# Issuing the next group's row products between the chunks of the present group's 5x5 convolution

## The chip, the cores and the metric

One core of one Trainium2 chip runs the whole program. The metric is device time in microseconds. The core is alone in the program, and the spread of one kernel's runs is about 0.2 %. PE is the matmul engine, PEld its weight loads, DVE the vector engine, ACT the scalar engine, POOL the GpSimd engine, SP the engine that issues loads.

## The reference, cut to what matters

The program is four layers: a row LSTM, an adder network, a Hartley transform, and an encoder-decoder. The change touches the encoder of the last layer, which handles 16 images of 32 channels in four groups of four images (one 32-partition block each):

```
b1 = norm(0.5 * corr(x, SOBEL_X) + 0.5 * corr(x, SOBEL_Y))     # and four more edge operators, b2 ... b5
y  = conv3x3(concat([b1, b2, b3, b4, b5]), conv1_w, conv1_b)   # 160 channels in, 32 out
y  = maxpool2(y)
y  = conv2 -> pool -> conv3 -> pool -> conv4 -> deconv1 -> conv5 -> deconv2 -> conv6 -> ...
```

`norm` divides by a standard deviation over the whole image. The kernel therefore needs the statistics of five filtered images before it can convolve. It never makes these images: their variances follow from products of rows of x with neighbouring rows (here "row products"). Filters, norms and conv1 are then folded into one 5x5 convolution with 32 input channels, plus corrections along the edges.

## The kernel before

The parts that the argument touches (cuts marked with [...]):

```python
def edge_statistics(nc, pool, ps, cst, gm, frames, g):
    gram = [ps.tile([128, 512], F32, name="acc") for _ in range(4)]      # four accumulator banks
    [...]
    for ch in range(H // 16):                                            # 8 chunks of 16 rows
        xp = frames.chunk(g, ch)
        for l in range(2, 18):                                           # row products: 16 small matmuls a row
            [...]
                    nc.tensor.matmul(gram[blk][...], xp[rows, l, ...], xp[rows, l : l + n, ...], ...)
    [...]                                                                # then DVE: es_w, es_red, means, deviations
    return mean, inv_sqrt(nc, pool, var, 5, 0.0), sides

def fold_operators(nc, pool, ps, cst, w1, mean, istd, bias):
    [...]
    for n, (...) in PARTS.items():              # n: all, t, tl, tr, b, bl, br, l, r
        t = pool.tile([128, h * w + 1, 32], F32, name=f"fo_{n}")
        nc.gpsimd.memset(t, 0.0)                                         # L634
        [...]                                   # some 170 small DVE instructions (L647, L650)
    b = pool.tile([128, 4], F32, name="fo_b")
    p = [ps.tile([128, 512], F32, name="acc") for _ in range(4)]         # four more banks
    [...]                                                                # bias products into p (L659)
    for blk in range(4):
        nc.vector.tensor_tensor(b[:, blk : blk + 1], p[blk][:, :1], bias[:, 0:1], ALU.add)   # L663
    return out, b

# encoder: fp has bufs=2, ps has bufs=8 (all eight banks, one name)
ready = prepared(0)                             # statistics and fold of group 0
for g in range(NG):
    sides, wf, b1 = ready
    if g + 1 < NG:
        ready = prepared(g + 1)                 # statistics and fold of the next group, before this convolution
    [...]                                       # side products, then `cut`
    for ch in range(H // R):                    # the 5x5 convolution, 8 chunks of 800 matmuls (L814)
        acc = [ps.tile([128, 512], F32, name="acc") for _ in range(4)]
        [...]                                   # then DVE and ACT add `cut`, pool, add the bias: the eviction
    conv_pool(y1, 64, "conv2", 1, y2)           # conv2 to conv6, with deconv1 and deconv2 between
    [...]
```

A buffer pool here has a set of buffers for each name: a tile waits until the tile that held its buffer before, under the same name, has had its last reader.

## Time and profile before

| | before |
|---|---|
| time, median of 3 runs | 9529.88 us (9524.95 to 9548.11) |
| profiled run | 9529.85 us, span 9528.1 us |
| encoder, from its first loads to the end of conv6 of the last group | 6738 to 8905.4 us of the span (first row product at 6765.7) |
| preparation before the first convolution | 386.1 us |
| group 0: from its convolution to the next one | 548.6 us |
| group 3: convolution, then conv2 to conv6 | 221.3 us, 87.0 us |

From the page of the kernel before: the span, two of the slice rows (tenths of busy time, tenths of full clock), and the two groups of PE instructions that the change moves (count, then busy us and mean ns, then the idle time just before them and what ended it):

```profile
span 9528.1 us, 263499 instructions
...
PE   4999979999999999999999999857549677689877
...
PEclk9999989999999999999999999555559688789888
...
L814 PE MATMUL acc<-xp,fo_all 32*32 32x512 f32 x25600 | 931.1, 624 | 55.2 <-DVE pooled L718 48.1
...
L559 PE MATMUL acc<-xp 32*32 32x108 f32 x16384 | 321.1, 370 | 260.1 <-issue 228.3
```

The row products (L559) are busy 321 us and cost another 228 us in which PE waited for nothing but its own instructions ("issue"). The convolution (L814) waits 48 us for pooling. Slices 26 to 30 run at half clock; the last two of them, from 6738 us on, are the preparation ahead of the first convolution. Slice 32, at 0.6, holds the next row products.

### The profile page before, as it was taken

The page shows a single profiled execution, that of the slowest core. Times are in us where ns is not written, and L with a number is a line of the kernel's source. Part 1 is how long each engine was busy: PE and PEld are TensorE (multiplying, and loading weights), DVE is VectorE, ACT ScalarE, POOL GpSimd, SP SyncE. Part 2 cuts the span into 40 slices and gives each one's busy share as a digit, 9 for nine tenths or more (in the row PEclk, how much of TensorE's full clock was granted, in tenths as well). Part 3 has the DMA queues.
Part 4 walks back from the last instruction along what each step waited for, and adds up shares of the span by engine and source line. Part 5 has one row for each costly group of instructions (what it writes and reads, how often), then busy time and mean ns, then how long its engine had stood idle before and what let it go on. Part 6 is the DMA issues. An engine that isn't in the chain of part 4 may idle for free.

```text
span 9528.1 us, 263499 instructions
## 1 busy us (share of the span) xinstructions
PE 8174.5 (86%) x122202; PEld 5240.3 (55%) x122202; DVE 6188.6 (65%) x7704; ACT 5079.5 (53%) x3286; POOL 478.9 (5%) x585
## 2 busy tenths in 40 slices
PE   4999979999999999999999999857549677689877
PEld 4888864544445444444544444856436455457544
DVE  5444439999999999999999999315252232322333
ACT  1444329989899898989989899000001101011200
POOL 0111110000000000000000000000000000000122
PEclk9999989999999999999999999555559688789888
DMA  9899930000000000000000000527411111111333
GB/s 193 61 80 80 61 55 1 19 19 19 19 10 11 19 19 19 20 19 1 19 19 20 19 10 7 161 48 229 145 52 41 55 35 46 46 30 34 103 119 112
DMA packets 1530826, 494.30 MB, mean 52 GB/s; under 512 B 1420028, under 2 KB 1423612, under 8 KB 1522172
## 3 DMA queue, kind: packets, MB, share of 16 engines
q1 hardware_dynamic: 1474588, 364.48, 23.3%
q10 hardware_dynamic: 55136, 112.95, 3.3%
q8 instruction: 957, 15.68, 0.7%
q14 instruction: 145, 1.19, 0.0%
HBM read 330.59 MB, written 146.80 MB: 50 GB/s over the span
## 4 chain that ended last, share of the span: by engine, by line
DVE 41%; PE 38%; issue 14%; DMA 3%; SPq 2%; ACT 1%; POOL 1%; DVEq 0%; ACTq 0%; POOLq 0%
DVE d_dve L317 34%; PE acc L814 9%; PE pg L179 4%; PE pg L180 4%; PE acc L559 3%; PE acc L705 3%; PE pg L181 2%; PE p L379 2%; PE acc L300 2%; PE acc L932 2%; PE pf L479 1%; PE acc L906 1%; DMA out_dram<-xo 1%; DVE xc L332 1%; PE acc L323 1%
## 5 line engine op out<-in xcount | busy, mean ns | idle before, releaser
L323 PE MATMUL acc<-d_dve,sel 128*32 128x512 f16 x27648 | 3994.0, 379 | 44.0 <-DVE d_dve L317 44.0
L323 PEld LDWEIGHTS <-sel 128*32 128x32 f16 x36864 | 2042.8, 95 | 2056.1 <-issue 218.4
L314 ACT ACTIVATE d_act<-qa,neg 128x4096 f16<-128x4096 f16 x768 | 2803.0, 3697 | 131.8 <-PE acc L323 131.1
L317 DVE TENSOR_SCALAR d_dve<-qa,qw 128x4096 f16<-128x4096 f16 x2304 | 2790.3, 1284 | 111.1 <-PE acc L323 86.5
L323 PE MATMUL acc<-d_act,sel 128*32 128x512 f16 x9216 | 2182.2, 380 | 0.0
L314 ACT ACTIVATE d_act<-qb,neg 128x4096 f16<-128x4096 f16 x384 | 1419.2, 3696 | 0.0
L317 DVE TENSOR_SCALAR d_dve<-qb,qw 128x4096 f16<-128x4096 f16 x1152 | 1411.4, 1284 | 0.0
L814 PE MATMUL acc<-xp,fo_all 32*32 32x512 f32 x25600 | 931.1, 624 | 55.2 <-DVE pooled L718 48.1
L814 PEld LDWEIGHTS acc<-xp,fo_all 32*32 32x32 f32 x25600 | 664.5, 105 | 313.8 <-issue 162.9
L179 PE MATMUL pg<-h,bd 128*128 128x256 f32 x2048 | 651.7, 400 | 59.8 <-DVE h L199 59.5
L190 ACT ACTIVATE gt<-pg,bias 128x256 f32<-128x256 f32 x1024 | 400.9, 474 | 546.1 <-PE pg L181 545.9
L180 PE MATMUL pg<-h,bd 128*128 128x256 f32 x2048 | 622.3, 386 | 0.0
L729 ACT ACTIVATE y<-pooled,fo_b 32x128 f32<-32x128 f32 x256 | 102.4, 400 | 841.0 <-DVE pooled L718 837.6
L559 PE MATMUL acc<-xp 32*32 32x108 f32 x16384 | 321.1, 370 | 260.1 <-issue 228.3
L842 DVE TENSOR_TENSOR acc<-acc,cut 128x4 f32<-128x4 f32 x256 | 28.7, 166 | 698.1 <-PE acc L814 697.1
L181 PE MATMUL pg<-xn,bd 128*128 128x2 f32 (+62 forms) x2048 | 425.6, 289 | 10.7 <-DVE xn L163 10.7
L181 PEld LDWEIGHTS pg<-xn,bd 128*128 128x128 f32 x2048 | 396.1, 194 | 67.6 <-DVE xn L163 11.5
L559 PEld LDWEIGHTS acc<-xp 32*32 32x32 f32 x16384 | 246.6, 133 | 334.3 <-issue 275.2
L180 PEld LDWEIGHTS pg<-h,bd 128*128 128x128 f32 x2048 | 397.9, 194 | 56.8
L194 DVE TENSOR_TENSOR c<-c,gt 128x256 f32<-128x256 f32 x256 | 108.5, 424 | 447.7 <-ACT gt L190 447.7
L530 DVE TENSOR_SCALAR xp<-xp,stats 128x2560 f32<-128x2560 f32 (+1 forms) x64 | 101.1, 1580 | 457.6 <-DMA xp<-x_d 457.6
L179 PEld LDWEIGHTS pg<-h,bd 128*128 128x128 f32 x2048 | 341.2, 195 | 66.8 <-issue 49.9
(233 smaller groups left out, 5879.5 us busy)
## 6 DMA issues: line engine op xcount, KB each, us to landing
xp<-x_d SPq DMA_DIRECT2D x48, 1280.0 KB
x_in<-in_x_dram SPq DMA_DIRECT2D x16, 2048.0 KB
res<-in_x_dram SPq DMA_DIRECT2D x32, 1024.0 KB
x_d<-res SPq DMA_DIRECT2D x32, 1024.0 KB
x_d<-xc ACTq DMA_DIRECT2D x16, 2048.0 KB
xr<-x_d SPq DMA_DIRECT2D x32, 1024.0 KB
x_d<-xr ACTq DMA_DIRECT2D x32, 1024.0 KB
xr<-x_d SPq DMA_DIRECT2D x128, 256.0 KB
```

The costliest lines, as they stand in the source:

```text
L179: nc.tensor.matmul(pg[:, q], wmat(0, q), h_in[:, :, 1:], start=True, stop=False)
L180: nc.tensor.matmul(pg[:, q], wmat(1, q), h_in[:, :, :H], start=False, stop=False)
L181: nc.tensor.matmul(pg[:, q, :, : t + 1], wmat(2, q), xn[:, 2 * c : 2 * c + 2, j, : t + 1], start=False, stop=True,)
L190: nc.scalar.activation(gt[:, q], pg[:, q], AF.Tanh if q == 3 else AF.Sigmoid, bias=bias[:, q : q + 1])
L300: nc.tensor.matmul(acc[k][32 * j : 32 * j + 32, :], sel16[:, 8, :], window(tap)[:, 4 * k : 4 * k + 4, :], start=tap == 0, stop=False,)
L314: nc.scalar.activation(d, window(tap), AF.Relu, bias=neg[:, i : i + 1])
L317: nc.vector.tensor_scalar(d, window(tap), qw[:, i : i + 1], 0.0, ALU.subtract, ALU.max)
L323: nc.tensor.matmul(acc[k][32 * j : 32 * j + 32, :], sel16[:, f8, :], ds[j][:, 4 * k : 4 * k + 4, :], start=False, stop=f8 == 7 and tap == 8,)
L379: nc.tensor.matmul(p1[:, i, :], xh[:, 16 * half + i, :], cst["cas"], start=True, stop=True)
L559: nc.tensor.matmul(gram[blk][32 * j : 32 * j + 32, at : at + 36 * n], xp[rows, l, 2 + 32 * j : 34 + 32 * j], xp[rows, l : l + n, 32 * j : ...
L705: nc.tensor.matmul(acc[blk][32 * j : 32 * j + 32, : rows * n], wc[name][part, tap, :], src[part, at : at + rows, kw : kw + n], start=tap == 0,
L814: nc.tensor.matmul(acc[blk][32 * j : 32 * j + 32, :], wf["all"][rows, tap, :], xp[rows, 4 * j + kh : 4 * j + kh + 4, kw : kw + W], start=t ...
```

## The change

The intent: the row products of the next group need only x, so they can be spread between the chunks of this group's convolution. PE then has work while a chunk is evicted, and the convolution of a group need not wait until the next group has been prepared. For this the row products get four banks of their own ("gram"), and the other tiles keep four ("acc").

```diff
-def edge_statistics(nc, pool, ps, cst, gm, frames, g):
+def edge_statistics(nc, pool, ps, cst, gm, frames, g, out):
-    gram = [ps.tile([128, 512], F32, name="acc") for _ in range(4)]
+    gram = [ps.tile([128, 512], F32, name="gram") for _ in range(4)]
[... in the loop over chunks, after a chunk's row products:]
+        yield
[... the statistics' and the fold's other PSUM tiles: "acc" -> "gram"]
-    return mean, inv_sqrt(nc, pool, var, 5, 0.0), sides
+    out.update(mean=mean, istd=inv_sqrt(nc, pool, var, 5, 0.0), sides=sides)
[...]
-        ps = ctx.enter_context(tc.tile_pool(name="e_ps", bufs=8, space=PSUM))
+        ps = ctx.enter_context(tc.tile_pool(name="e_ps", bufs=4, space=PSUM))
[...]
-            if g + 1 < NG:
-                ready = prepared(g + 1)
+            following = Operators(g + 1) if g + 1 < NG else None
[... after each chunk of the convolution:]
+                if following:
+                    following.step()
+            if following:
+                ready = following.folded()
             conv_pool(y1, 64, "conv2", 1, y2)
```

`Operators` holds the generator. `step()` issues one chunk of row products. `folded()` runs what is left (the statistics, then the fold), after the whole convolution.

More of the change, by code (lines that the diff above doesn't have):

```diff
@@ L589, in edge_statistics @@
         nc.vector.tensor_reduce(red[:, blk, :], w, AX.X, ALU.add)
-    p = ps.tile([128, 512], F32, name="acc")
+    p = ps.tile([128, 512], F32, name="gram")
     nc.tensor.matmul(p[:, :20], cst["ones"], red[:, 0:4, :].rearrange("p b k -> p (b k)"), start=True, stop=True)
@@ L595, in edge_statistics @@
     nc.vector.tensor_reduce(sq, own.rearrange("p b k -> p k b"), AX.X, ALU.add)
-    q = ps.tile([128, 512], F32, name="acc")
+    q = ps.tile([128, 512], F32, name="gram")
     nc.tensor.matmul(q[:, :5], cst["avg32_bc"], red[:, 4, :], start=True, stop=True)
@@ L654, in fold_operators @@
     b = pool.tile([128, 4], F32, name="fo_b")
-    p = [ps.tile([128, 512], F32, name="acc") for _ in range(4)]
+    p = [ps.tile([128, 512], F32, name="gram") for _ in range(4)]
     for j in range(4):
@@ L766, in deconv, with __init__, step, folded @@
                     )
-        def prepared(g):
-            mean, istd, sides = edge_statistics(nc, fp, ps, cst, gm, frames, g)
-            return sides, *fold_operators(nc, fp, ps, cst, w1, mean, istd, bias)
-        ready = prepared(0)
+        class Operators:
+            def __init__(self, g):
+                self.out = {}
+                self.steps = edge_statistics(nc, fp, ps, cst, gm, frames, g, self.out)
+            def step(self):
+                next(self.steps, None)
+            def folded(self):
+                for _ in self.steps:
+                    pass
+                o = self.out
+                return o["sides"], *fold_operators(nc, fp, ps, cst, w1, o["mean"], o["istd"], bias)
+        ready = Operators(0).folded()
         for g in range(NG):
             sides, wf, b1 = ready
-            if g + 1 < NG:
-                ready = prepared(g + 1)
+            following = Operators(g + 1) if g + 1 < NG else None
             cps = [ps.tile([128, 512], F32, name="acc") for _ in range(4)]
```

## The prediction

> **What bounds the kernel now.** I read the page's slices first. The change touches only the encoder, slices 29 to 37; the 40 slices are 238 us each, and everything before 6738 us and after 8905 us of the span is the same code in both kernels. Then I cut the encoder into its stages with the table by windows (PE's busy time, then the granted clock):
>
> ```profile
> 6738.00:7124.06 386.06, 174.51 (x8968) 0.50 0.27 76
> 7124.06:7386.34 262.28, 245.93 (x6736) 0.92 0.14 37
> 7386.34:7480.52 94.18, 77.95 (x2042) 0.84 0.06 17
> 7480.52:7621.73 141.21, 79.03 (x4110) 0.55 0.29 82
> 7621.73:7672.65 50.92, 9.87 (x742) 0.50 0.10 28
> ...
> 8597.07:8818.41 221.34, 214.72 (x6745) 0.99 0.10 27
> 8818.41:8905.39 86.98, 73.70 (x2040) 0.86 0.01 3
> ```
>
> From the top: row products and folding of groups 0 and 1; the 5x5 convolution of group 0; its conv2 to conv6; the row products of group 2 (141 us, PE half busy at half clock); their tail (51 us, PE nearly idle). The last two lines are the 5x5 convolution and conv2 to conv6 of group 3, which has no follower. So a group takes 548.6 us (7124.06 to 7672.65), 192 of them preparation that PE could partly do elsewhere. That is what the change is after. Two things in the table are odd: the row products run at half clock, and the convolution of group 3 is 41 us shorter than that of group 0. The timeline of PE explains both. Row products (start, us, then the idle time before):
>
> ```profile
> 7485.00 1.77 PE L559 MATMUL acc<-xp 32*32 32x108 f32 x128 [1.84 <-issue]
> 7489.02 1.77 PE L559 MATMUL acc<-xp 32*32 32x108 f32 x128 [2.25 <-issue]
> ...
> 7508.66 2.55 PE L559 MATMUL acc<-xp 32*32 32x108 f32 x128 [1.19 <-issue]
> ...
> 8046.42 2.54 PE L559 MATMUL acc<-xp 32*32 32x108 f32 x128 [5.56 <-issue]
> ...
> 8059.30 2.54 PE L559 MATMUL acc<-xp 32*32 32x108 f32 x128 [0.93 <-issue]
> ```
>
> Every 128 matmuls (256 instructions with their weight loads) PE stops. At full clock 128 take 1.77 us, at half clock 2.54, but the period is the same, 3.5 to 3.75 us: a faster clock only lengthens the stop. The row products are bound by the supply of instructions, not by the array. The long stops (3 to 5.6 us) coincide with loads of xp.
>
> The 5x5 convolution (800 matmuls a chunk), group 0, then what holds its banks:
>
> ```profile
> 7189.08 1.88 PE L814 MATMUL acc<-xp,fo_all 32*32 32x512 f32 x18 [1.26 <-DVE pooled L718]
> ...
> 7192.08 28.92 PE L814 MATMUL acc<-xp,fo_all 32*32 32x512 f32 x782 [1.12 <-DVE pooled L718]
> ...
> 7394.78 0.35 DVE L663 TENSOR_TENSOR fo_b<-acc,bias 128x1 f32<-128x1 f32 x4
> ```
>
> Each chunk waits for the pooling of the chunk just finished, as if there were four banks and not eight. The other four hold the bias products of the next group, whose reader L663 runs only at 7394.78, after the whole convolution. So groups 0 to 2 take 262.3/8 = 32.8 us a chunk, and group 3 (eight banks) 221.3/8 = 27.7 us.
>
> **What the Trainium skill says.** "Runtime: NRT & Kernel Launch", section "Instruction fetch mechanics": instructions come in 16 KiB blocks of 256, and the cost of crossing a block is "mostly hidden". The trace agrees with the 256 and not with hidden: 0.93 us at least, 5.56 at most, at each block of row products. "TensorE: Matmul & The Clock Gate", section "What's actually happening": the array runs at half clock after an idle window and at full clock after about 3.4 us of sustained work. The windows agree roughly: granted 0.50 in the tail, full about 3 us after the convolution starts at 7124; entering the row products at 7480.5 it stays at 1.00 until about 7493. "PSUM — Partial Sum Buffer", "The four PSUM rules": a matmul's output lies in one bank, and there are eight. 4 + 4 is therefore all of it.
>
> **The change part by part.** No arithmetic is removed. In the built instruction order of the changed kernel I see: 256 row products (512 matmul records) after each convolution chunk; those of chunk 0 of the group after next spread over conv2 to conv6; the side products L791 after conv6; and, on DVE, the whole statistics and fold of the next group between the last chunk's eviction and the first pooling of conv2.
>
> Start-up: only group 0 is prepared first. Its fold ended at 6964.6, fo_l at 6961. Side products follow (704 records, 5.5 blocks of 3.7 us, 20 us), so its convolution starts near 6980 instead of 7124: 144 us earlier.
>
> A chunk: eviction takes 6 us of DVE and now lies under the row products. Convolution warm about 26 us (25.09 us for 766 records in group 3), plus some 2 us for a restart at half clock in most chunks: 28. Row products: 512 records at 13.8 ns = 7.1, 3.5 stops of 1.85 = 6.5, a load of xp in the way, 2: 15.5, estimated. Sum 43.5, against 32.8 + 130/8 = 49. The interleaving earns only about 5.5 us a chunk, because the stops for instructions go along.
>
> From the last convolution matmul of groups 0 to 2 to the end of conv2: before 27 us (7386.3 to 7413.3). After: last row products 15.5; es_w and es_red 18.7; the rest of the fold 36.6 (in group 0 the tail took 6909.4 to 6964.6, 55.2 in all); only then does DVE pool conv2's first half, and with four banks its second half waits: 16 more. Together 87 us. Only conv2's first half (11 us) is hidden under the 55 us tail; the rest of it is still exposed.
>
> conv3 to conv6: 67.5 us before (7413.3 to 7480.8); 6 more for conv6's second half, which must wait for four banks, and 6 more for hosted row products in groups 0 and 1: 79.5, 79.5, 73.5. Side products: before in the shadow of the fold in groups 1 and 2, now bare, as they were for group 3:
>
> ```profile
> 8579.78 1.47 PE L791 MATMUL acc<-sides,fo_l 32*32 32x32 f32 x128 [1.63 <-issue]
> ...
> 8593.21 1.53 PE L791 MATMUL acc<-sides,fo_r 32*32 32x32 f32 x128 [4.41 <-issue]
> ...
> 8597.07 3.98 PE L814 MATMUL acc<-xp,fo_all 32*32 32x512 f32 x58
> ```
>
> From the end of conv6 at 8576 to that start is 21 us.
>
> Sum: group 0: 8 x 28 + 7 x 15.5 + 87 + 79.5 + 21 = 520. Group 1, with one chunk of row products hosted: 8 x 28 + 5.9 x 15.5 + 87 + 79.5 + 21 = 503. Group 2: 497. Together 1520, against 1473 before (7124.06 to 8597.07). So convolution 3 starts at 6980 + 1520 = 8500 instead of 8597, 97 us earlier. It then runs with four banks, as group 0 did before: 262.3 for 221.3, 41 lost. Its conv2 and conv6 lose some 10 us too. Net 97 - 41 - 10 = 46 us gained: 9529.9 - 46 = 9484 us.
>
> **The rivals.** (a) The whole preparation disappears: 141 + 51 us for each of groups 2 and 3 and 144 at the start, some 500 us, giving about 9030. It would need a PE with empty slots between chunks. Against it: PE is 94% busy in the convolution (245.93 of 262.28) and the row products' period does not shrink at full clock. For it: idle eviction gaps of some 3 us a chunk, which are filled. (b) The four banks and the DVE tail ahead of conv2 cost more than is won: if row products take 18 us a chunk and every restart 4 us, the 24 chunks lose 24 x 4.5 = 108 us against my sum, giving about 9590. For it: the 5.56 us stops, and two loads of xp per period. (c) The clock stays full through the row products, because 128 matmuls at full clock keep PE about half busy, as from 7480.5 to 7493: then the 2 us restart goes and row products come nearer 14: 24 x 3.5 = 84 us less, about 9400. (d) A transfer becomes the wait. A load lands in some 9 us and has a whole period of 43 us; I give this little.
>
> **Range and chances.** The uncertain terms are the row products per chunk (14 to 17), the restart (0 to 4), and the 87 us. The first two each move some 35 to 45 us over 22 to 24 chunks, the third some 20 a group; combined about 55. So 9410 to 9555 for 8 in 10. Two per cent is 190 us: faster needs nearly half of rival (a), slower needs worse than (b).
>
> **What would show it.** Right: row products between chunks still in blocks of 128 with a period near 3.6 us though the clock is higher; PE idle for about 30 us inside conv2 of groups 0 to 2, released by es_red and then by pooling; no wait for pooling in chunks of groups 0 to 2, but one in group 3, whose convolution takes about 262 us; L791's successor bare for some 20 us. Wrong: blocks of row products without stops next to the convolution (supply caught up), or conv2's pooling running ahead of the fold, or waits of PE for xp.

## The result

| | before | changed |
|---|---|---|
| median | 9533.4 us (4 runs, 9524.95 to 9548.11) | 9568.35 us (4 runs, 9565.52 to 9583.03) |
| ratio | 1 | 1.0038, 95% interval 1.0021 to 1.0056 |

Ratios are the mean time of one kernel's fast runs over that of the other's fast runs of the same rounds, so not quite the ratio of the medians. The change is 0.4 % slower: within 2 %, but 84 us from my 9484, with the other sign than the gain of 46 us that I forecast, and outside the range of 9410 to 9555. On another chip, with other runs, the changed kernel had the same ratio (below).

The page of the changed kernel, the same lines as above:

```profile
span 9581.0 us, 263456 instructions
...
PE   4999979999999999999999998947476877869777
...
PEclk9999989999999999999999999555588887879888
...
L827 PE MATMUL acc<-xp,fo_all 32*32 32x512 f32 x25600 | 933.0, 634 | 40.3 <-issue 20.6
...
L560 PE MATMUL gram<-xp 32*32 32x108 f32 x16384 | 316.0, 330 | 301.2 <-issue 226.8
```

The half-clock stretch is one slice shorter and the clock in the middle is higher. Yet the row products, now L560, cost the same: busy plus waiting for instructions is 316.0 + 226.8 = 542.8 us, and it was 321.1 + 228.3 = 549.4. A single product did become shorter (330 for 370 ns); the sum did not follow. The convolution's busy time, now L827, is unchanged too (933.0 for 931.1).

The stages of the changed kernel, by windows (PE's busy time, then the granted clock):

```profile
6741.70:6983.89 242.19, 91.47 (x4840) 0.51 0.27 75
6983.89:7332.90 349.01, 289.56 (x10277) 0.88 0.20 55
7332.90:7421.40 88.50, 41.44 (x1178) 0.65 0.12 32
7421.40:7530.04 108.64, 80.53 (x2726) 0.77 0.10 35
...
8584.46:8848.07 263.61, 245.59 (x6736) 0.92 0.08 23
8848.07:8954.20 106.13, 88.83 (x2040) 0.82 0.01 3
```

From the top: the preparation of group 0; its convolution with seven chunks of row products of group 1; from its last convolution matmul to the end of conv2; conv3 to conv6 and the side products of group 1; then the convolution and conv2 to conv6 of group 3. The first window is 143.9 us shorter than its counterpart, as intended. All of that is given back. Group 0, from the start of one convolution to the next, takes 349.0 + 88.5 + 108.6 = 546.1 us (548.6 before), although it no longer contains a preparation stretch; groups 1 and 2 take 526.0 and 528.5. Together this is 1600.6 us, where I had summed 1520 and the kernel before has 1473.0. Group 3's convolution starts at 8584.46 instead of 8597.07 and is then 42.3 us longer (263.61 against 221.34), its conv2 to conv6 19.1 us longer (106.13 against 86.98). (A convolution ends here where conv2 begins, as in the windows of the prediction.)

One chunk's row products, then the convolution (PE's timeline: start, us, then the idle time before):

```profile
7060.03 3.00 PE L560 MATMUL gram<-xp 32*32 32x108 f32 x193
7068.31 2.54 PE L560 MATMUL gram<-xp 32*32 32x108 f32 x128 [5.28 <-issue]
7071.78 2.54 PE L560 MATMUL gram<-xp 32*32 32x108 f32 x128 [0.93 <-issue]
7075.53 1.20 PE L560 MATMUL gram<-xp 32*32 32x108 f32 x48 [1.20 <-issue]
7076.49 8.35 PE L827 MATMUL acc<-xp,fo_all 32*32 32x512 f32 x199
7086.16 19.20 PE L827 MATMUL acc<-xp,fo_all 32*32 32x512 f32 x589 [1.32 <-issue]
```

The stops after each 128 matmuls are there as before. They sum to 7.4 us in this chunk, and the row products take 7076.49 - 7060.03 = 16.5 us in all. The stop of 5.28 us falls together with a load of xp (the windows show 127 to 207 GB/s from 7060 to 7068) and lets the clock fall to half, so that the convolution starts cold: its first 199 matmuls take 8.35 us, 42 ns each, the next 589 take 33 ns each.

What PE waits for in these stops can be read from the trace itself. Its page has a DMA queue for instructions (q8 in the kernel before: 957 packets, 15.68 MB, so 16 KiB a packet; PE's 244404 matmuls and weight loads are 955 blocks of 256). I went through the packets of this queue in the kept trace: in the kernel before 125 stops of over 0.8 us ahead of a row product, in the changed kernel 100, each have a packet of their own, and PE resumes 1.2 to 1.6 us after that packet has ended. So "issue" means here that the next block of instructions had not yet come.

After the convolution, inside conv2 of group 0, on PE and then on DVE:

```profile
7383.73 2.21 PE L707 MATMUL acc<-y,w_conv 32*32 32x512 f32 x28
7406.89 0.70 PE L560 MATMUL gram<-xp 32*32 32x108 f32 x6 [20.95 <-DVE fo_b L665]
7407.79 13.91 PE L707 MATMUL acc<-y,w_conv 32*32 32x512 f32 x281 [0.20 <-DVE pooled L720]
...
7407.05 1.28 DVE L720 TENSOR_REDUCE pooled<-acc 128x128 f32<-128x512 f32 x2
```

The first half of conv2 is done before 7386; the second waits 21 us, until DVE has finished the whole fold (its last instruction is L665, the bias) and pools. Behind conv6, the side products lie bare:

```profile
7510.36 1.72 PE L804 MATMUL acc<-sides,fo_l 32*32 32x32 f32 x128 [3.29 <-issue]
...
7530.04 5.53 PE L827 MATMUL acc<-xp,fo_all 32*32 32x512 f32 x102
```

They began at 7504.4 and the convolution follows at 7530.0: 25.7 us with PE mostly waiting for instructions. Conv6 had ended at 7500.5; the side products first wait until its last results have been evicted. From the end of conv6 to the next convolution it is 29.6, 26.4 and 25.8 us in groups 0 to 2. In group 3, where all eight banks used to serve the convolutions, conv6 is now in two parts. In the kernel before it is one unbroken run:

```profile
8886.50 18.88 PE L705 MATMUL acc<-d,w_conv 32*32 32x512 f32 x576
```

In the changed kernel its second half has to wait for the eviction of the first, and starts with six matmuls that take 3.81 us:

```profile
8938.31 3.81 PE L707 MATMUL acc<-d,w_conv 32*32 32x512 f32 x6 [3.83 <-DVE y L729]
8942.49 11.62 PE L707 MATMUL acc<-d,w_conv 32*32 32x512 f32 x282 [0.37 <-DVE y L729]
```

### The profile page after: what moved, and what is told of

Read it like the earlier page. It is cut to its first block, busy times and chain, and to the rows that moved or that the text cites. A ratio compares the mean times of both kernels' runs of the same rounds, so it can differ in the third digit from the quotient of the medians.

```text
span 9581.0 us, 263456 instructions
## 1 busy us (share of the span) xinstructions
PE 8191.2 (85%) x122202; PEld 5215.8 (54%) x122202; DVE 6187.7 (65%) x7704; ACT 5079.1 (53%) x3286; POOL 476.2 (5%) x585
## 4 chain that ended last, share of the span: by engine, by line
DVE 41%; PE 38%; issue 14%; DMA 3%; SPq 2%; ACT 1%; POOL 1%; DVEq 0%; ACTq 0%; POOLq 0%
DVE d_dve L317 33%; PE acc L827 9%; PE pg L179 4%; PE pg L180 4%; PE gram L560 3%; PE acc L707 3%; PE pg L181 2%; PE p L379 2%; PE acc L300 2%; PE acc L949 2%; PE pf L479 1%; PE acc L923 1%; DMA out_dram<-xo 1%; DVE xc L332 1%; PE acc L323 1%
## 5 line engine op out<-in xcount | busy, mean ns | idle before, releaser
L827 PE MATMUL acc<-xp,fo_all 32*32 32x512 f32 x25600 | 933.0, 634 | 40.3 <-issue 20.6
L827 PEld LDWEIGHTS acc<-xp,fo_all 32*32 32x32 f32 x25600 | 650.4, 106 | 295.6 <-issue 148.5
L560 PE MATMUL gram<-xp 32*32 32x108 f32 x16384 | 316.0, 330 | 301.2 <-issue 226.8
L560 PEld LDWEIGHTS gram<-xp 32*32 32x32 f32 x16384 | 246.1, 122 | 364.6 <-issue 310.3
```

Source lines behind the costliest of these rows:

```text
L560: nc.tensor.matmul(gram[blk][32 * j : 32 * j + 32, at : at + 36 * n], xp[rows, l, 2 + 32 * j : 34 + 32 * j], xp[rows, l : l + n, 32 * j : ...
L827: nc.tensor.matmul(acc[blk][32 * j : 32 * j + 32, :], wf["all"][rows, tap, :], xp[rows, 4 * j + kh : 4 * j + kh + 4, kw : kw + W], start=t ...
```

## The experiments

Theory A says: the row products are bound by the supply of instructions, so they cost the same wherever they are issued, and the interleaving hides only what the evictions leave idle; on top of that the split of the banks and the position of the tail (statistics and fold ahead of conv2) cost more than this. Its rivals: the tail alone carries the loss; the split of the banks alone carries it; or the gain lay in something that the kernel before did wrong and that has nothing to do with interleaving. Ten runs were made (one of them of the changed kernel again), on three chips, each with its own runs of the kernel before: 9521.64 us in the first, 9530.02 in the second, 9525.4 in the third.

**Half as many row products.** In the changed kernel:

```diff
-        for l in range(2, 18):
+        for l in range(2, 18, 2):
-                        gram[blk][32 * j : 32 * j + 32, at : at + 36 * n],
+                        gram[blk][32 * j : 32 * j + 32, at : at + 72 * n],
-                        xp[rows, l : l + n, 32 * j : 32 * j + 36],
+                        bcast(xp[rows, l : l + n, 32 * j : 32 * j + 36], 2, 2),
```

Every product is twice as wide, because its columns are read twice, and there are half as many, because every second row is left out. So the sums are wrong.

> The changed kernel with half as many row products, each over twice the columns (216 instead of 108), so the array streams as many columns as before and the instructions halve. The result is wrong on purpose. Theory A (instruction supply bounds the row products, wherever they stand): a chunk's row products fall from about 16.5 to about 8.5 us, the time from 9568 to about 9310 us (32 chunks by 8). Theory B (the array's own work or the half clock bounds them): the time stays within 30 us of 9568.

REFUSED: the wrong sums gave the square root a negative number (-0.408) in the check before the chip, so this never ran. The mended version adds 100 to the variances:

```diff
-    out.update(mean=mean, istd=inv_sqrt(nc, pool, var, 5, 0.0), sides=sides)
+    out.update(mean=mean, istd=inv_sqrt(nc, pool, var, 5, 100.0), sides=sides)
```

> The changed kernel with half as many row products, each over twice the columns (216 instead of 108), so the array streams as many columns as before and the instructions halve; a constant is added under the square root because the wrong sums would make it negative. The result is wrong on purpose. Theory A (instruction supply bounds the row products, wherever they stand): a chunk's row products fall from about 16.5 to about 8.5 us, the time by about 240 us (32 chunks by 7 to 8), to about 9320. Theory B (the array's own work or the half clock bounds them): the time stays within 30 us of the changed kernel's 9560.

Measured: 9337.92 us, ratio 0.9799 (0.9785 to 0.9814). Against the changed kernel that is 1.0038 - 0.9799 = 2.4 %, some 228 us for 8192 instruction pairs fewer. In its table of groups the row products read:

```profile
L560 PE MATMUL gram<-xp 32*32 32x216 f32 x8192 | 209.7, 389 | 171.7 <-issue 97.2 <-DVE fo_b L665 41.9 <-ACT xp L535 32.3
```

The array did as much work (half the products, each with twice the columns), but the wait for instructions fell from 226.8 to 97.2 us and the busy time from 316.0 to 209.7. The convolutions of groups 0 to 2 with their row products took 293, 285 and 281 us, where they had taken 349, 333 and 332. (The 41.9 us are two waits for the end of the fold inside conv2, as the one at 7406.89 in the changed kernel, and stand in both.) So the number of instructions sets their cost far more than the width. The instruction queue agrees: 893 packets where the changed kernel has 956, and 228 us for 63 packets are 3.6 us each, close to the period of the blocks. The comparison with the reference passed this version, although its sums are wrong: its tolerance does not see these statistics, and a "correct" says little about them.

**Fold after conv3.** In the changed kernel, to let conv2 be pooled before the fold:

```diff
-            if following:
-                ready = following.folded()
             y2, y3 = padded(32, "y2"), padded(16, "y3")
             conv_pool(y1, 64, "conv2", 1, y2)
             conv_pool(y2, 32, "conv3", 2, y3)
+            if following:
+                ready = following.folded()
```

> The changed kernel with the statistics and fold of the next group written after conv3 instead of before conv2. Theory A (37 us of fold on DVE stand in front of conv2's first pooling and PE waits for them): the stretch from the last convolution matmul to the end of conv2 falls from 88 us to about 50 and the time by some 110 us, to about 9460. Theory B (DVE's fold only moves into conv4 to conv6, whose chain is as tight): within 30 us of 9568.

Measured: 9510.37 us, ratio 0.9991 (0.9976 to 1.0006): 0.47 % better than the changed kernel, some 45 us, and less than half of what I expected. The stretch from the last convolution matmul to the end of conv2 did fall as Theory A says, from 88 to some 52 us, but conv3 to conv6 grew from some 79 to 96 to 100. The trace says why: the DVE instructions were not executed where the program text put them. The fold ran from 7354 to 7384, still ahead of conv2's second pooling, and conv3 waited for it (PE's timeline):

```profile
7384.63 11.26 PE L707 MATMUL acc<-y,w_conv 32*32 32x256 f32 x278 [20.37 <-DVE pooled L720]
```

The same wait stands in groups 1 and 2 (20.41 us each). The exposed tail was moved behind the next convolution and is shorter there, not hidden.

**All eight banks for the last group.** In the changed kernel, where the row products are over in group 3, its accumulators take turns between the two sets:

```diff
+        def bank_name():
+            turn["n"] += 1
+            return "gram" if turn["last"] and turn["n"] % 2 else "acc"
-                acc = [ps.tile([128, 512], F32, name="acc") for _ in range(4)]
+                which = bank_name()
+                acc = [ps.tile([128, 512], F32, name=which) for _ in range(4)]
[... the same for conv2 to conv6 and the deconvolutions; turn["last"] = following is None]
```

> The changed kernel, but in group 3, which has no follower, the convolutions take the four idle row-product banks by turns with their own. Theory A (four banks cost group 3 what eight had given): its 5x5 convolution falls from 265 to about 222 us and its conv2 to conv6 from 105 to about 87, so 60 us in all, to about 9508. Theory B (the lower speed of group 3 comes from something else, clock or transfers): no change, 9568.

Measured: 9478.22 us, ratio 0.9957 (0.994 to 0.9973): 0.81 % better than the changed kernel, some 77 us, where I had expected 60. The convolution of group 3 took 216 us instead of 264 (144 of its 6400 matmuls had already run in the gaps of group 2's conv2 to conv6), conv2 to conv6 88 instead of 106. This part of the loss is therefore shown to come from the split of the banks.

**The split without the interleaving.** In the kernel before:

```diff
-    gram = [ps.tile([128, 512], F32, name="acc") for _ in range(4)]
+    gram = [ps.tile([128, 512], F32, name="gram") for _ in range(4)]
[... the statistics' and the fold's other PSUM tiles likewise; e_ps bufs=8 -> bufs=4]
```

> The kernel before with the change's split of the banks alone, four for row products and folding and four for everything else, and no interleaving. Theory A (the split itself costs, the interleaving earns): group 3's convolution 262 us instead of 221, conv2 to conv6 of each group about 105 us instead of 87 to 94, so 42 + 18 + 3 x 11 = about 93 us slower than before, 9615; then the interleaving alone is worth about 55 us. Theory B (the split is free where banks were held anyway, and the interleaving is what loses): within 30 us of before.

Measured: 9597.56 us, ratio 1.0069 (1.0054 to 1.0084). The split alone costs 0.69 %, some 66 us. The convolution of group 3 now waits at every chunk, as those of groups 0 to 2 did (PE's timeline):

```profile
8664.18 1.88 PE L814 MATMUL acc<-xp,fo_all 32*32 32x512 f32 x18 [1.25 <-DVE pooled L718]
8667.17 28.77 PE L814 MATMUL acc<-xp,fo_all 32*32 32x512 f32 x782 [1.12 <-DVE pooled L718]
```

It takes 262.9 us (8599.2 to 8862.1), and conv2 to conv6 take 108.3. The first three groups together, from the start of the first convolution to that of the last, take 1476.5 us (1473.0 before), so nearly all of the loss lies in group 3. The difference to the changed kernel, 1.0069 - 1.0038 = 0.31 %, some 30 us (the two intervals just touch), is all that interleaving earns on top of the split.

**Another name for the bias tile, in the kernel before.** The prediction says that the reader of the bias products, L663, runs only after the whole convolution. It does not ask why. The timelines of DVE and of POOL in the kernel before answer it:

```profile
7384.94 3.30 DVE L647 SCALAR_TENSOR_TENSOR fo_b<-fo_ws,fo_b 128x96 f32<-128x96 f32 x19 [25.03 <-POOL fo_b L634]
...
7384.51 0.39 POOL L634 MEMSET fo_b<- 128x352 f32 x1 [23.83 <-PE acc L831]
```

The fold of the next group clears its weights for the bottom edge ("fo_" plus "b") only when this group's last chunk has multiplied with its own (L831, the edge products). There are two buffers for each name, so this should not happen. But the bias tile is also called fo_b: each group takes two buffers of that name, and the next group has none left until the convolution is over. L663 lies behind this on DVE, and so four banks are held throughout the convolution. The edit is one word:

```diff
-    b = pool.tile([128, 4], F32, name="fo_b")
+    b = pool.tile([128, 4], F32, name="fo_bias")
```

> The kernel before, with one name changed: the folded bias gets a tile name of its own instead of sharing the name, and so the two buffers, of the fold's bottom-edge weights. Theory A (the shared name makes the bias of the next group wait for the end of the present convolution, and so holds four of eight banks through it): no wait for pooling between chunks in groups 0 to 2, their convolutions fall from 262 to about 222 us, the time to about 9410. Theory B (the name has nothing to do with it, the four banks are held for another reason): 9530, same waits.

Measured: 9391.82 us, ratio 0.9867 (0.9852 to 0.9882), correct, some 127 us faster than before. The bias is now read at 7116, just after the convolution's start at 7113, and the convolution runs through a border of chunks without a stop (the view ends at 7200):

```profile
7153.53 47.08 PE L814 MATMUL acc<-xp,fo_all 32*32 32x512 f32 x1410 [2.29 <-issue]
```

The convolution of group 0 takes 224.6 us instead of 262.3, those of groups 1 and 2 224.7 and 224.0, with no wait for pooling. Unchanged order and renamed tile: row products of one group 137 us (7428.6 to 7565.3), a convolution 225 us, together 362. Interleaved: 368 us (6983.9 to 7351.5), the eighth chunk of row products included. Two stretches that are issued one after the other with free banks take no longer than the two interleaved.

**The tail under the convolution, with all eight banks.** From the changed kernel: names back to "acc" with 8 buffers, the bias tile renamed, the row products gathered in one block ahead of the convolution as before, and the tail issued under its first chunks. ScalarE copies the sums to SBUF, so that the banks are free at once:

```diff
+    gs = pool.tile([128, 4, GRAM], F32, name="es_gram", bufs=1)
+    for blk in range(4):
+        nc.scalar.copy(gs[:, blk, :], gram[blk][:, :GRAM])
+    yield
[... es_w reads gs]
             following = Operators(g + 1) if g + 1 < NG else None
+            if following:
+                following.gather()                     # all row products
[... after the chunks of the convolution:]
-                if following:
+                if following and ch == 0:
                     following.step()                   # the statistics
-            if following:
-                ready = following.folded()
+                if following and ch == 1:
+                    ready = following.folded()
```

> A version meant to beat both: row products of the next group stay before the convolution as in the kernel before, with eight banks and the bias under its own name; ScalarE copies the four row-product banks to SBUF, and the statistics and the fold are issued after the first and the second chunk of the present convolution, where DVE is idle. Theory A (what could be hidden all along was DVE's 51 us tail, not PE's row products): the convolutions of groups 0 to 2 take about 222 us, no 51 us gap before them, side products bare for some 20 us: against the kernel before about 41 x 3 + 31 x 3 = some 215 us less, about 9310. Theory B (the tail on DVE gets in the way of the evictions, and PE waits at the chunks instead): no better than the renamed kernel's 9392.

Measured: 9382.46 us, ratio 0.9848 (0.9832 to 0.9864), correct. I had expected 9310. From the start of the first convolution to that of the last it is no better than the rename (1353.3 us against 1341.4). The fold is one block of some 33 us on DVE, and the pooling of the next chunk stands behind it, once a group (first the run after the stop, then the convolution's line in the table of groups of the encoder):

```profile
7170.30 39.97 PE L837 MATMUL acc<-xp,fo_all 32*32 32x512 f32 x1060 [12.53 <-DVE pooled L724]
...
L837 PE MATMUL acc<-xp,fo_all 32*32 32x512 f32 x25600 | 868.4, 610 | 65.9 <-DVE pooled L724 39.0 <-issue 26.9
```

**The fold in pieces.** The last kernel, but the fold is a generator too, and hands out 24 of its DVE instructions after each chunk:

```diff
                     nc.vector.scalar_tensor_tensor(d, s, sign * op[ur][uc], d, ALU.mult, ALU.add)
+                    count += 1
+                    if count % 24 == 0:
+                        yield
[... after each chunk:]
-                if following and ch == 0:
+                if following:
                     following.step()
-                if following and ch == 1:
-                    ready = following.folded()
+            if following:
+                ready = following.folded()
```

> The eight-bank version with the tail under the convolution, but the fold's DVE instructions are handed out in pieces of 24 between the evictions of chunks 1 to 7 instead of all at once after chunk 1. If the 12.5 us wait per group for the pooling of chunk 1 is what kept that version (9382) from its expected 9310, then each of groups 0 to 2 loses that wait and the clock restart behind it: 3 x 15 = 45 us, so about 9340, and no chunk waits over 2 us for pooled. Rival: the four banks held by the bias products and the DVE instructions between evictions hold up the chunks anyway, only in smaller waits: 9375 to 9390.

Measured: 9347.6 us, ratio 0.981 (0.9794 to 0.9827), correct: the fastest correct version, ahead of both kernels. The waits for pooling are gone from the same table:

```profile
L846 PE MATMUL acc<-xp,fo_all 32*32 32x512 f32 x25600 | 854.6, 607 | 31.6 <-issue 31.5
```

The convolutions of groups 0 to 2 take 231, 229 and 230 us (248, 243 and 247 before this edit), and the sum of the three groups is 1311.7 us against 1353.3. The wait was the cause.

**Both mended costs of the changed kernel at once.** Eight banks for the last group and the fold after conv3; the edits are those shown above.

> The changed kernel with both of its mended costs at once: group 3 takes its accumulators from both sets of four banks, and the fold is issued after conv3. If the two costs are independent, their separate gains (0.81 % and 0.47 % of the time) add: ratio to before about 1.0038 - 0.0081 - 0.0047 = 0.991, some 9445 us. If they overlap (both work on conv2 to conv6), 0.993 to 0.996. Either way it should stay behind the unchanged order with the bias tile renamed (0.9867).

Measured: 9463.64 us, ratio 0.9933 (0.9919 to 0.9948). The gains come to 1.05 % where their sum is 1.28 %. The gap of 0.23 % is no larger than the intervals of these ratios allow (some 0.15 % each way), so whether the two costs overlap stays open. The mended interleaving beats the kernel before by 0.7 % and stays behind the one-word edit.

**The changed kernel again**, on one chip with the fold in pieces, both mended costs and the run after this one:

> The changed kernel again, beside the others on one chip, to have its ratio there: 1.002 to 1.006.

Measured: 9562.58 us, ratio 1.0038 (1.0023 to 1.0053). The result holds.

**The changed kernel with the bias tile renamed.** The same one-word edit.

> The changed kernel with only the bias tile renamed. In it the fold is issued after the whole convolution, so nothing of the fold can wait for a tile that the convolution still reads: the rename should do nothing here, ratio to before 1.002 to 1.006 as without it. If it is faster by over 0.5 %, the shared name also costs the changed kernel time, in a wait that I have not seen.

Measured: 9569.52 us, ratio 1.0045 (1.003 to 1.006): nothing gained. By its order the changed kernel is free of that wait. Part of what it wins is thus, by this argument, the cure of a fault that it does not know of.

## Why the prediction was wrong

The ledger, each term of the sum against its measurement in the profiled run:

| term | predicted, us | measured, us |
|---|---|---|
| start of the first convolution | 6980 | 6983.9 |
| convolution with row products, groups 0 / 1 / 2 | 332.5 / 315.5 / 315.5 | 349.0 / 333.1 / 332.4 |
| last convolution matmul to the end of conv2 | 87 each | 88.5 / 87.6 / 90.6 |
| conv3 to conv6 with side products | 100.5 / 100.5 / 94.5 | 108.6 / 105.3 / 105.5 |
| group 3's convolution with four banks | 262.3 | 263.6 |
| group 3's conv2 and conv6, extra | 10 | 19.1 |

(For the second row I leave the last chunk's row products to the third, as the 87 us contain them: 8 x 28 + 7 x 15.5 = 332.5, and 5.9 chunks in groups 1 and 2.) The misses in order are 3.9, 51.0, 5.7, 23.9, 1.3 and 9.1 us, together 95. The rest of the program, the same code, was 4 us longer in this run. That leads from 9484 to the profiled 9583. The profiled run is the slowest of the four, 15 us above their median, so some 15 us of this ledger is spread between runs that I can't assign to a term.

**Right: the row products are bound by the supply of instructions.** The stops stay, the sum of busy time and stops is the same (542.8 for 549.4 us), and half as many products remove 228 us from the whole; each stop ends after a packet of instructions of its own. Three details of the reading were loose: one of the full-clock lines shown has a period of 4.02 us, not 3.5 to 3.75; the shortest regular stops are 0.89 us; and that the long stops coincide with loads of xp holds only in part (after 6984 in the changed kernel the DMA engines were busy 44 % in the 21 stops over 3 us and 22 % in 49 shorter ones, but in four of the long ones under 25 %). **Right: the exposed tail**, 87 us predicted and 88 to 91 measured. **Right: four banks make group 3's convolution as slow as the others were**, 262 predicted, 264 measured, and taken back by the alternating banks (216). **Right: side products bare behind conv6**, though not their length (below). **Right: rival (a), that the preparation disappears, fails.** Rival (c) shows in part and earns nothing: the clock stays full at the start of the row products (1.00 from 7060) and falls to half at the long stop (0.50 from 7068), and they take no less time. Rival (d) does not show: no wait for a load stands among PE's waits from the first convolution to the end of the encoder.

**Wrong: the step "Convolution warm about 26 us [...] plus some 2 us for a restart [...]: 28", taken eight times.** This is the step that failed: the chunks took 29.6, 30.0 and 29.8 us on average in groups 0, 1 and 2 (237, 240 and 239 us for eight, cut where PE's timeline changes between convolution and row products), so 13, 16 and 15 of the some 17 us that each of the three convolutions missed. I took the 26 us from an inner chunk of group 3. The first and the last chunk have extra edge products, some 3.5 us each, which I left out. The six inner chunks took 29.0, 29.8 and 28.9 us on average; why they exceed 28 stays open. The row products took 15.8 to 16.0 us a chunk and not 15.5, another 2 to 3 us a group (the 16.5 us of the chunk shown are above their mean).

**Wrong: "6 more for conv6's second half" and "some 10 us".** Both are the cost of four banks in the stages after the convolution. In group 3 I put 10 us on it and measured 19.1; the split alone, without interleaving, showed 108.3 - 87.0 = 21.3. The mechanism, a second half that waits for the first half's banks, was the one named. Each wait costs more than its idle time: 3.83 us idle, then 3.81 us for six matmuls. In groups 0 to 2, conv3 to conv6 took 79.1, 78.9 and 79.7 us, where I had 79.5, 79.5 and 73.5. Group 2 hosts no row products and takes as long, so the banks cost 12 us and not 6, and the hosted row products nothing and not 6: in groups 0 and 1 two errors cancelled, which was luck.

**Wrong: the 21 us of the side products.** That was group 3's figure in the kernel before, with all banks free. Measured from the end of conv6 to the next convolution it was 29.6, 26.4 and 25.8 us, so 19 of the 24 us that the fourth row missed. Some 3.9 us of each come from a wait that I had not named: the side products begin only when conv6's last results have been evicted (L804, released by DVE y L729). The rest, 4.7, 1.5 and 0.9 us, is not broken down.

So each mechanism was right, and but for this wait no new one came; the terms were mis-sized, nearly all in the same direction. The sign came out wrong because the sum is a small difference of large terms: I predicted a start of group 3 that is 97 us earlier and 51 us lost there, and got 12.6 us earlier (16 without the later start of the encoder in that run), 61 us lost there, and 4 us more in the rest. My range took the misses as independent and put them at 55 us. Eight chunks in three groups share one estimate, and its error counts 24 times in the same direction. Rival (b) had this arithmetic, with 4.5 us a chunk for 108 us; what came was 51 us, plus the bank costs and the side products.

**What I had not seen at all** lies in the kernel before. I took "as if there were four banks and not eight" as a property of the schedule. It was one name for two tiles. With that undone, the order of before is 127 us faster, and the interleaving has nothing left to earn: 362 us one after the other against 368 us interleaved. My sum compared the interleaving with a convolution that was 38 us too slow in each of three groups.

**My expectations for experiments failed twice** (and the half-products run, at 9338 for 9320, was near). For the late fold I assumed that program text decides the place of DVE's instructions; the trace shows the fold inside conv2 all the same. For the tail under the convolution I counted 31 us a group (the tail of 51 less 20 for the side products) as hidden and forgot that pooling stands in the same queue; in pieces, it came within 8 us of its expectation.

## What to carry to other kernels

When work is bound by the number of its instructions, moving it next to other work on the same engine hides nothing: count its time as busy plus "issue", and see whether a faster clock changes that sum before moving it. When an engine waits as if it had half its buffers, follow the chain to the instruction that holds them, and past it to what that waits for, before designing around the shortage; here it ended at two tiles that shared a name. An estimate per chunk that is used 24 times should be checked on the odd chunks too, and its error multiplied, not averaged.

## What the Trainium skill lacked or had wrong

- "Runtime: NRT & Kernel Launch", section "Instruction fetch mechanics": it calls the cost of crossing a block of 256 instructions "mostly hidden". For small matmuls it is not: 226.8 us of stops in the row products of the changed kernel, up to 5.82 us each, and 129.6 us less (97.2) with half as many products; each of the 100 over 0.8 us ended 1.2 to 1.6 us after a packet of the instruction queue. Its text gives PE room for 2048 instructions and its note speaks of two lines only; with the larger size one would expect several blocks without a stop after a rest, but in the kernel before PE stopped 2.27 us at the next block after 12.07 us of idle time (at 7107.33).
- "TensorE: Matmul & The Clock Gate", section "What's actually happening": the two states and the fall after an idle window agree with the trace (a stop of 5.28 us, then a granted clock of 0.50). It does not say how long full clock lasts at about half duty; entering the row products from conv6, the kernel before kept 1.00 from 7480.5 to about 7494, with PE about half busy.
- No page that I read says that two tiles of one pool under one name share their buffers, or how such a wait looks in a trace. Here it was worth 127 us, and it looks like an engine that waits for a memset (25.03 us, released by POOL).
